# Summing softmax exponentials in place with an adding DMA, GpSimd adds and a fold, in a fused attention and feed-forward kernel

## Chip, cores and metric

The kernel runs on one core of one Trainium2 chip. The metric is device time in microseconds (us) of one execution; the program is launched once for the whole computation.

## What is computed

The reference is a pre-norm transformer block on `x` of 8 x 1024 x 512 in float32: differential attention with 16 heads, then a feed-forward part with ternary weights.

```python
qkv = layernorm(x) @ w_qkv                     # 16 heads of 32; q and k are split in halves of 16
a1 = softmax(q1 @ k1.T / sqrt(32)); a2 = softmax(q2 @ k2.T / sqrt(32))
out = (a1 - lam * a2) @ v                      # then RMS norm per head, norm_w, times 0.2
x = x + rearranged(out) @ wo
h = bitlinear(layernorm(x), w_fc) + gate * (x @ v.T @ fast_b.T @ u.T)
x = x + bitlinear(relu(h) ** 2, w_proj)
```

The change concerns the denominators of the two softmaxes: for each query, the sum over 1024 keys of the exponentials of one map.

## The kernel before

**Stages.** A first stage (to about 140 us of the span) normalises and projects batch 0 and prepares the ternary weights. The attention loop runs to about 4260 us. The feed-forward part takes the rest and is not touched.

**Units.** The attention loop is cut into NU = 256 units: batch, head, and half of the 1024 queries (HS = 512). 32 units make a batch. For one unit the scores stand with keys on the partitions: 8 chunks of 128 keys (`kc` = 0 to 7), two maps (`sm`) and 512 queries. The loop goes two chunks at a time, so a unit has four steps, called here by their first chunk: kc 0, 2, 4 and 6. I write (u, kc) for a step.

**What a step does**, in the order written by hand, which TensorE (PE), ScalarE (ACT), VectorE (DVE) and GpSimd (POOL) keep as it stands:

- `max_scores` (L207, L218): score products of the unit two ahead (AHEAD = 16 chunks), whose row maxima DVE takes out of three PSUM banks.
- `exp_scores` (L267, L273): for the unit itself, minus the maximum (from `nms`) plus the scores on PE, and the exponential on ACT into a tile `e` of 128 x 2 x 2 x 512 float32, 1 MB. One `e` tile holds the two chunks of a step, so a unit has four: e0 to e3, in the dictionary `e_of[u, kc // 2]`.
- `add_up` (L283, L285): GpSimd adds tiles into a separate tile `es`: es = e0 + e1 at kc 2, es += e2 at kc 4, es += e3 at kc 6.
- extra work, gathered in `posts`: at kc 0 a step of `fill` (for the next batch: normalised rows, transposes L137, values L145, projections L157), `max_turn` (L232: transposes the next unit's maxima and sends them through DRAM to `nms`), `heads_out` (L324: transposes and divides the results of an earlier unit), and `sums`. In the second half of a batch every fourth unit has one more projection at kc 4. Every fourth unit has an output projection of four units (`output_rows`, L383) at kc 4, one unit after `rms_apply` (L368 to L371) on GpSimd at kc 2.
- `values` (L290): the products with the values for the two chunks of the step before, that is, one step late.

**Sums.** `sums(v)` multiplies by a matrix of ones: `quarters` issues four small products of 256 columns for each part of 512 keys-by-query columns. A part is half a tile (one of two chunks). `es` is two parts; a unit that is `light` leaves e3 out of the GpSimd adds and sums it as two more parts on PE. Light are 17 of the last 32 units (the odd ones and the last three). `sums(v)` stands at (v + 2, 0), for light units at (v + 1, 2); `heads_out(v)` at (v + 3, 0), for light units at (v + 2, 0).

**Buffers.** Five `e` tiles and two `es` tiles are turned round in order: a new `e` tile is the one used five tiles before, and its writer waits until the last reader of that one is done. PSUM has three banks for the maxima, one for the values and four (`one_bank`) for all else. GpSimd issues no DMA in this loop; SyncE (SP) issues them all.

Of the kernel before, what the change touches and what calls it, by code (L numbers as in the profile page):

```python
# [8 lines left out]
F32 = mybir.dt.float32  # L9
F32R = mybir.dt.float32r  # L10
AF = mybir.ActivationFunctionType
ALU = mybir.AluOpType
# [5 lines left out]
P = 128  # L18
# [6 lines left out]
def block_phases(  # L25
# [14 lines left out]
    nc = tc.nc  # L40
    B, S, E = x.shape
    H, HD = norm_w.shape
# [3 lines left out]
    HS = S // 2  # L46
    SCALE = float(HD) ** -0.5
    NU = B * H * 2
# [55 lines left out]
    def one_bank():  # L104
        return ps_1.tile([P, 512], F32, tag="one", name="one")
# [71 lines left out]
    def load_keys(g):  # L177
        b, h = divmod(g, H)
        tk_of[g] = p_tk.tile([P, S], F32R, tag="tk", name="tk")
        src = qk_of[b][1, h * HD : (h + 1) * HD]  # L180
        for i in range(2):
            nc.sync.dma_start(
                tk_of[g][i::2].bitcast(F32), src[:, i : i + 1, :].to_broadcast([HD, 2, S])
            )

    def load_queries(u):
        b, h = divmod(u // 2, H)
        cols = slice((u % 2) * HS, (u % 2) * HS + HS)
        tq_of[u] = p_tq.tile([P, HS], F32R, tag="tq", name="tq")
        src = qk_of[b][0, h * HD : (h + 1) * HD, :, cols].rearrange("r i t -> (r i) t")  # L190
        for i in range(2):
            nc.sync.dma_start(tq_of[u][i::2].bitcast(F32), src)
# [37 lines left out]
    def max_turn(u):  # L230
        tr = one_bank()
        nc.tensor.transpose(tr[0:8, 0:P], nm2_of.pop(u), ident)  # L232

        def post():
            mt = p_s.tile([8, 2, P], F32R, tag="mt", name="mt", bufs=2)
            nc.vector.tensor_copy(mt[:, 0, :], tr[0:8, 0:P])
            nc.vector.tensor_sub(mt[:, 1, :], tr[0:8, 0:P], mt[:, 0, :].bitcast(F32))
            md = dpool.tile([2, 4, 2, P], F32, tag="md", name="md", bufs=4)
            nc.sync.dma_start(md.rearrange("s c a t -> (s c) a t"), mt.bitcast(F32))
            for sm in range(2):  # L240
                nc.sync.dma_start(
                    nms[u % 3][64 * sm : 64 * sm + 2].bitcast(F32)
                    .rearrange("a (c t) -> a c t", c=4),
                    md[sm].rearrange("c a t -> a c t"),
                )

        return post

    e_of, es_of, acc_of, avs_of = {}, {}, {}, {}

    def exp_scores(u, kc, between=None):

# [19 lines left out]

    def light(u):

        return u >= NU - 2 * H and (u % 2 == 1 or u >= NU - 3)

    def add_up(u, kc):
        e = e_of[u, kc // 2]  # L280
        if kc == 2:
            es_of[u] = p_es.tile([P, 2, 2, HS], F32, tag="es", name="es")
            nc.gpsimd.tensor_add(es_of[u], e_of[u, 0], e)  # L283
        elif kc == 4 or kc == 6 and not light(u):
            nc.gpsimd.tensor_add(es_of[u], es_of[u], e)  # L285

    def quarters(out, w, e, start, stop):

        for g in range(4):
            nc.tensor.matmul(  # L290
                out[32 * g : 32 * g + 32, :], w,
                e[:, g // 2, (g % 2) * (HS // 2) : (g % 2 + 1) * (HS // 2)],
                start=start, stop=stop,
            )
# [10 lines left out]
    def evict(u):  # L305
        avs_of[u] = p_s.tile([P, 2, HS // 2], F32, tag="avs", name="avs", bufs=4)

        nc.scalar.activation(avs_of[u][:, 0, :], acc_of.pop(u), AF.Copy, scale=one_nlam)

    def sums(u):  # L310
        ps = one_bank()
        es = es_of.pop(u)
        parts = [t[:, i] for t in ((es, e_of[u, 3]) if light(u) else (es,)) for i in range(2)]
        for i, part in enumerate(parts):
            quarters(ps[:, 0 : HS // 2], ones, part, i == 0, i == len(parts) - 1)
        return lambda: nc.scalar.copy(avs_of[u][:, 1, :], ps[:, 0 : HS // 2])
# [39 lines left out]
    def rms_squares(n):  # L356
        sq_of[n] = p_y.tile([P, 4, P], F32, tag="sq", name="sq")
        nc.scalar.activation(sq_of[n], og_of[n], AF.Square)
# [16 lines left out]
    def output_rows(n, bank=one_bank):  # L375
        b, hp = divmod(n, NHP)
        xr = p_y.tile([P, E], F32, tag="xr", name="xr")
        rows = x[b].rearrange("(d r) e -> r d e", d=HD)
        for r in range(4):
            nc.sync.dma_start(xr[32 * r : 32 * r + 32, :], rows[4 * hp + r])  # L380
        py = bank()
        for c in range(KC):
            nc.tensor.matmul(  # L383
                py, og_of[n][:, c, :], wo_sb[:, c, :],
                start=(c == 0), stop=(c == KC - 1),
            )

        def post():
            y = p_y.tile([P, E], F32, tag="y", name="y")
            nc.vector.scalar_tensor_tensor(y, py, nw[:, hp : hp + 1], xr, ALU.mult, ALU.add)  # L390
            nc.sync.dma_start(x1_dram[n // 4][n % 4], y)

        return post
# [39 lines left out]
    def whole(step):  # L433
        post = step()
        if post:
            post()
# [3 lines left out]
    with tc.tile_pool(name="a_stage", bufs=1) as stage, tc.manual_schedule(engines=engines):  # L440
# [26 lines left out]
        for i, step in enumerate(steps):  # L467
# [4 lines left out]
            posts = [step()]  # L472
# [7 lines left out]
            if i >= heads:  # L480
                um, im = divmod(i - heads, NS)
# [71 lines left out]

    adds, outs = {}, {}
    for v in range(NU):
        adds.setdefault((v + 1, 2) if light(v) else (v + 2, 0), []).append(v)
        outs.setdefault((v + 2, 0) if light(v) else (v + 3, 0), []).append(v)
    done = None
    ctx.enter_context(tc.manual_schedule(engines=engines))
    with tc.tile_pool(name="a_e", bufs=5) as p_e, tc.tile_pool(name="a_es", bufs=2) as p_es:  # L560
        for s in range(0, NS * NU + 2, 2):
            u, kc = divmod(s, NS)
            um, im = divmod(s + AHEAD, NS)
            if done is not None:
                evict(done)
                done = None
            if u > NU - 2 * H and kc == 0:
                prep.fetch()
            if um < NU:
                if im == 0 and um + 1 < NU:  # L570
                    if um % 2 == 1:
                        load_keys(um // 2 + 1)
                    load_queries(um + 1)
                between, first = max_scores(um, im, apart=True)
            else:
                between = first = None
            if u < NU:
                if u % (2 * H) == 0 and kc == 0:
                    assert not fill
                    fill = prepare(u // (2 * H) + 1) if u + 2 * H < NU else prepare_tokens()  # L580
                exp_scores(u, kc, between=between)
                if first:
                    first()
                exp_scores(u, kc + 1)
                add_up(u, kc)
            reduce = max_scores(um, im + 1) if um < NU else None
            posts = []

            if fill and (kc == 0 or kc == 4 and u % (2 * H) >= H and u % 4 == 0):
                prepare_step, long = fill.pop(0)  # L590
            else:
                prepare_step = None
            if prepare_step and long:
                posts.append(prepare_step())
            if kc == 0 and um <= NU:
                posts.append(max_turn(um - 1))
            for v in outs.pop((u, kc), []):
                posts.append(heads_out(v))
                if v % 4 == 3:
                    n = v // 4  # L600
                    later[u, 6] = lambda n=n: rms_squares(n)
                    later[u + 1, 0] = lambda n=n: rms_sums(n)
                    later[u + 1, 2] = lambda n=n: rms_apply(n)
                    later[u + 2, 4] = lambda n=n: output_rows(n)
            if (u, kc) in later:
                posts.append(later.pop((u, kc))())
            for v in adds.pop((u, kc), []):
                posts.append(sums(v))
            if prepare_step and not long:
                posts.append(prepare_step())  # L610
            if reduce:
                reduce()
            if 2 <= s < NS * NU + 2:
                uv, kv = divmod(s - 2, NS)
                values(uv, kv)
                values(uv, kv + 1)
                if kv == NS - 2:
                    done = uv
            for post in posts:
                if post:  # L620
                    post()
        evict(done)
        prep.fetch_rest()
        whole(lambda: sums(NU - 1))
    assert not later and list(adds.values()) == list(outs.values()) == [[NU - 1]]

# [439 lines left out]
```

## Time and profile before

| | |
|---|---|
| median of 3 runs | 5345.61 us (5343.15 to 5349.25) |
| profiled execution: its own time | 5346.45 us |
| profiled execution: span of its instructions | 5344.5 us |
| granted TensorE clock | 0.999 |
| busy in the span: PE, DVE, ACT, POOL | 99%, 71%, 53%, 77% |
| DMA | 328.49 MB, mean 61 GB/s |

The profiler gives each instruction's start and duration. A group in the page is a line, an engine and an operation with its tiles, its count, its busy time and the mean of one in ns, then the idle time before it and what ended that. PE time is modelled for the ends of the matmuls, so 99% doesn't mean that PE has no slack. A timeline row is start, duration, engine, line, operation, tiles and shape. I divide the attention loop by batch: seven first halves (units 0 to 15 of batches 0 to 6), with transposes and values for the next batch as fill; seven second halves, with projections as fill; and the last batch, nearly without fill.

### The profile page before, as it was taken

Reading aid. Unit: us, or ns where it says so; the run is one execution under the profiler, and the core shown is the slowest. Engines: PE = TensorE matmul, PEld = TensorE weight load, DVE = VectorE, ACT = ScalarE, POOL = GpSimd, SP = SyncE. Lnnn points to the kernel's source line nnn. Section 1 sums busy time; section 2 is a strip of 40 time slices with the busy share of each in tenths; the row PEclk is TensorE's granted clock in tenths of the full one; section 3 lists DMA queues with packets and bytes.
Section 4 is the critical chain, followed back from the end, with each engine's and each line's share of the span. In section 5 each row is a group of like instructions: output and inputs, shape, how many; then the busy total and the mean of one; then the engine's idle time right before and its main releaser. Section 6 shows DMA issues by size and latency. Waiting matters only on the chain.

```text
span 5344.5 us, 105614 instructions
## 1 busy us (share of the span) xinstructions
PE 5277.1 (99%) x41522; PEld 3244.8 (61%) x41522; DVE 3786.5 (71%) x7599; ACT 2834.1 (53%) x5502; POOL 4128.1 (77%) x1511
## 2 busy tenths in 40 slices
PE   8999999999999999999999999999999999999999
PEld 4555555555555555555555555555555588788887
DVE  6877787777778777877777777777888545555554
ACT  4665566566656665666566656655666522222221
POOL 0998899889988998899899989998888733333333
PEclk9999999999999999999999999999999999999999
DMA  8112211221121112111211121112211101111111
GB/s 275 49 52 77 69 51 54 75 71 50 55 79 63 52 55 77 64 55 59 77 59 53 63 74 61 52 65 77 97 48 47 60 18 32 32 32 32 32 32 32
DMA packets 185247, 328.49 MB, mean 61 GB/s; under 512 B 33312, under 2 KB 55840, under 8 KB 184112
## 3 DMA queue, kind: packets, MB, share of 16 engines
q1 hardware_dynamic: 183824, 319.12, 18.7%
q8 instruction: 329, 5.39, 0.4%
q0 software_dynamic: 544, 2.10, 0.1%
q14 instruction: 166, 1.36, 0.1%
q10 hardware_dynamic: 384, 0.52, 0.0%
HBM read 209.16 MB, written 112.46 MB: 60 GB/s over the span
## 4 chain that ended last, share of the span: by engine, by line
PE 80%; POOL 12%; DVE 2%; issue 2%; ACT 1%; DMA 1%; SPq 0%; POOLq 0%; DVEq 0%; ACTq 0%
PE acc L290 15%; PE one L267 13%; PE mx L207 12%; PE one L157 8%; PE y L722 7%; POOL es L285 7%; PE pf L708 7%; PE one L290 4%; PE one L145 4%; PE one L383 3%; POOL es L283 3%; PE one L324 2%; DVE nm L218 1%; PE pf L709 1%; ACT e L273 1%
## 5 line engine op out<-in xcount | busy, mean ns | idle before, releaser
L218 DVE TENSOR_REDUCE nm<-mx 128x1 f32<-128x512 f32 x4096 | 2548.4, 682 | 257.6 <-PE mx L207 252.1
L273 ACT ACTIVATE e<-one 128x512 f32<-128x512 f32 x4096 | 2116.8, 602 | 802.8 <-PE one L267 750.5
L285 POOL TENSOR_TENSOR es<-es,e 128x2048 f32<-128x2048 f32 x495 | 2262.6, 4571 | 62.0 <-ACT e L273 30.0
L207 PE MATMUL mx<-tk,tq 64*128 64x512 f32 x4096 | 1451.2, 444 | 6.7 <-DVE nm L218 5.5
L283 POOL TENSOR_TENSOR es<-e 128x2048 f32<-128x2048 f32 x256 | 1170.0, 4570 | 277.1 <-ACT e L273 277.1
L267 PE MATMUL one<-nms,one 64*128 64x512 f32 x4096 | 1177.4, 420 | 4.6 <-ACT e L273 2.7
L290 PE MATMUL acc<-e,v 128*32 128x256 f32 x16384 | 1092.6, 384 | 0.0
L207 PEld LDWEIGHTS mx<-tk,tq 64*128 64x128 f32 x4096 | 751.0, 184 | 546.9 <-DVE nm L218 311.5
L267 PE MATMUL one<-tq,tk 64*128 64x512 f32 x4096 | 1065.0, 393 | 0.0
L712 POOL TENSOR_TENSOR r<-r 128x512 f32<-128x512 f32 x256 | 269.0, 1052 | 644.4 <-ACT r L711 636.7
L290 PEld LDWEIGHTS acc<-e,v 128*32 128x32 f32 x16384 | 450.1, 109 | 433.7 <-issue 177.3
L267 PEld LDWEIGHTS one<-tq,tk 64*128 64x128 f32 x4096 | 580.4, 185 | 83.2
L711 ACT ACTIVATE r<-pf,s_fc 128x512 f32<-128x512 f32 x256 | 176.5, 689 | 793.1 <-PE pf L709 555.8
L267 PEld LDWEIGHTS one<-nms,one 64*128 64x128 f32 x4096 | 515.8, 184 | 79.9 <-DVE og L347 14.7
L722 PE MATMUL y<-wpr,r 128*128 128x512 f32 x2048 | 523.7, 397 | 3.3 <-DVE r L716 1.5
L715 DVE CAST r<-r 128x512 fp32r<-128x512 f32 x256 | 179.0, 699 | 421.9 <-POOL r L712 421.8
L157 PE MATMUL one<-hT,wqk 128*128 128x512 f32 x1024 | 472.8, 605 | 0.0
L722 PEld LDWEIGHTS y<-wpr,r 128*128 128x128 f32 x2048 | 374.8, 188 | 98.6 <-DVE o L732 20.1
L708 PE MATMUL pf<-hTh,wfc 128*128 128x512 f32 x1024 | 399.3, 390 | 0.0
L708 PE MATMUL pf<-hTl,wfc 128*128 128x512 f32 x1024 | 398.9, 390 | 0.0
L165 DVE SCALAR_TENSOR_TENSOR pc<-one,pc 128x512 fp32r<-128x512 f32 x128 | 88.5, 691 | 344.4 <-ACT pc L164 344.4
L157 PEld LDWEIGHTS one<-hT,wqk 128*128 128x128 f32 x1024 | 184.1, 189 | 213.9 <-issue 186.4
(133 smaller groups left out, 4291.6 us busy)
## 6 DMA issues: line engine op xcount, KB each, us to landing
qk<-pc SPq DMA_DIRECT2D x128, 512.0 KB
tk<-qk SPq DMA_DIRECT2D x256, 256.0 KB
tq<-qk SPq DMA_DIRECT2D x512, 128.0 KB
xs<-in_L_attn_x SPq DMA_DIRECT2D x64, 256.0 KB
xr<-in_L_attn_x SPq DMA_DIRECT2D x256, 64.0 KB
x_dram<-y SPq DMA_DIRECT2D x64, 256.0 KB
out<-o SPq DMA_DIRECT2D x248, 64.0 KB
nms<-md SPq DMA_DIRECT2D x512, 4.0 KB
```

The costliest lines, as they stand in the source:

```text
L145: nc.tensor.matmul(pv, hT_of[b][:, kc, c * P : (c + 1) * P], wv[:, kc, :], start=(kc == 0), stop=(kc == KC - 1),)
L157: nc.tensor.matmul(ps, wqk[:, kc, c0 : c0 + P], hT_of[b][:, kc, tok], start=(kc == 0), stop=(kc == KC - 1),)
L207: nc.tensor.matmul(mx[sm], tq[rows, c * P : (c + 1) * P], tk[rows, kh * 512 : kh * 512 + 512], start=True, stop=True,)
L218: nc.vector.tensor_reduce(nm_of[u][:, kh, sm, c : c + 1], mx[sm], AX.X, ALU.max, negate=True)
L267: nc.tensor.matmul(st[sm], w[rows, cols], m[rows, :], start=(w is one2), stop=(w is not one2))
L273: nc.scalar.activation(e[:, kc % 2, sm, :], st[sm], AF.Exp)
L283: nc.gpsimd.tensor_add(es_of[u], e_of[u, 0], e)
L285: nc.gpsimd.tensor_add(es_of[u], es_of[u], e)
L290: nc.tensor.matmul(out[32 * g : 32 * g + 32, :], w, e[:, g // 2, (g % 2) * (HS // 2) : (g % 2 + 1) * (HS // 2)], start=start, stop=stop,)
L708: nc.tensor.matmul(pf, w[:, kc, :], hT, start=(kc == 0 and i == 0), stop=False)
L712: nc.gpsimd.tensor_mul(r, r, r)
L722: nc.tensor.matmul(ys[i], r2[:, i * P : (i + 1) * P], prep.wpr[j // (NJ // 2)][:, j % (NJ // 2), :], start=(j == 0 and k == 0), stop=(j == ...
```

## The change

`add_up` no longer uses a tile of its own. For most units, e1 += e0 is done at (u, 4) by a DMA that adds into its destination, issued by GpSimd. At (u, 6) GpSimd adds e2 += e3, then e2 += e1 (after the DMA has landed), then folds e2's second chunk onto its first. `sums` then has one part of four products instead of two. Light are only the last five units: they have e1 += e0 at kc 4 and e2 += e1 at kc 6 on GpSimd, and four parts on PE. `add_up` now stands at the end of the step behind `values`, since the in-place adds overwrite what `values` reads. `sums(v)` moves from (v + 2, 0) to (v + 1, 6), `heads_out(v)` from (v + 3, 0) to (v + 2, 0), and with it the RMS norm and the output projection by one unit. There are seven `e` tiles and no `es` tiles. Within kc 0, `heads_out` and `max_turn` go ahead of the fill step.

```diff
-        return u >= NU - 2 * H and (u % 2 == 1 or u >= NU - 3)
+        return u >= NU - 5
     def add_up(u, kc):
-        e = e_of[u, kc // 2]
-        if kc == 2:
-            es_of[u] = p_es.tile([P, 2, 2, HS], F32, tag="es", name="es")
-            nc.gpsimd.tensor_add(es_of[u], e_of[u, 0], e)
-        elif kc == 4 or kc == 6 and not light(u):
-            nc.gpsimd.tensor_add(es_of[u], es_of[u], e)
+        if kc == 4:
+            if light(u):
+                nc.gpsimd.tensor_add(e_of[u, 1], e_of[u, 1], e_of[u, 0])
+            else:
+                nc.gpsimd.dma_start(e_of[u, 1], e_of[u, 0], accum_op=ALU.add)
+        elif kc == 6:
+            e = e_of[u, 2]
+            if not light(u):
+                nc.gpsimd.tensor_add(e, e, e_of[u, 3])
+            nc.gpsimd.tensor_add(e, e, e_of[u, 1])
+            if not light(u):
+                nc.gpsimd.tensor_add(e[:, 0], e[:, 0], e[:, 1])
...
-        es = es_of.pop(u)
-        parts = [t[:, i] for t in ((es, e_of[u, 3]) if light(u) else (es,)) for i in range(2)]
+        parts = [e_of[u, 2][:, 0]]
+        if light(u):
+            parts += [e_of[u, 2][:, 1], e_of[u, 3][:, 0], e_of[u, 3][:, 1]]
...
-        adds.setdefault((v + 1, 2) if light(v) else (v + 2, 0), []).append(v)
-        outs.setdefault((v + 2, 0) if light(v) else (v + 3, 0), []).append(v)
+        adds.setdefault((v + 1, 2) if light(v) else (v + 1, 6), []).append(v)
+        outs.setdefault((v + 2, 0), []).append(v)
...
-    with tc.tile_pool(name="a_e", bufs=5) as p_e, tc.tile_pool(name="a_es", bufs=2) as p_es:
+    with tc.tile_pool(name="a_e", bufs=7) as p_e:
...
                 exp_scores(u, kc + 1)
-                add_up(u, kc)
...
-            if prepare_step and long:
-                posts.append(prepare_step())
-            if kc == 0 and um <= NU:
-                posts.append(max_turn(um - 1))
             for v in outs.pop((u, kc), []):
                 posts.append(heads_out(v))
...
+            if kc == 0 and um <= NU:
+                posts.append(max_turn(um - 1))
+            if prepare_step and long:
+                posts.append(prepare_step())
...
                 values(uv, kv + 1)
                 if kv == NS - 2:
                     done = uv
+                if u < NU:
+                    add_up(u, kc)
```

## The prediction on record

> **What bounds the kernel now.** I read the page's busy shares first, then busy time by window for one cycle of four units in each of the three kinds of stage, then the GpSimd and TensorE timelines of a cycle.
>
> The windows' columns are start:end, length, busy time of each engine with instruction counts, granted clock, DMA share, GB/s. The rows are a first half, a second half, and the last batch.
>
> ```profile
> 1268.90:1331.20 62.30, 62.30 (x566) 35.30 (x565) 49.39 (x102) 40.64 (x79) 60.97 (x22) 1.00 0.17 53
> 991.00:1061.80 70.80, 70.80 (x582) 39.68 (x584) 50.91 (x104) 39.98 (x79) 58.84 (x15) 1.00 0.23 76
> 4070.50:4128.70 58.20, 56.99 (x574) 33.22 (x576) 47.66 (x99) 37.20 (x74) 49.88 (x14) 1.00 0.16 48
> ```
>
> TensorE is full in all three. GpSimd (fifth figure) is full too in the first half, 60.97 of 62.30, and has room in the other two. So work taken off TensorE pays only where GpSimd lets it.
>
> GpSimd in the first half, from the timeline:
>
> ```profile
> 1292.22 4.52 POOL L283 TENSOR_TENSOR es<-e 128x2048 f32<-128x2048 f32 x1
> 1296.82 0.20 POOL L368 TENSOR_SCALAR ss<-ss 128x16 f32<-128x16 f32 x1
> 1297.11 2.92 POOL L369 TENSOR_TENSOR ss<-ss,neg_half 128x16 f32<-128x16 f32 x1
> 1300.11 1.05 POOL L371 TENSOR_TENSOR og<-og,ss 128x512 f32<-128x512 f32 x1
> 1301.12 9.19 POOL L285 TENSOR_TENSOR es<-es,e 128x2048 f32<-128x2048 f32 x2
> ```
>
> Three adds of 4.6 us a unit, and in every fourth unit 4.3 us of RMS norm between them.
>
> TensorE in one unit with only transposes as fill, from its timeline:
>
> ```profile
> 1274.13 0.50 PE L207 MATMUL mx<-tk,tq 64*128 64x512 f32 x1
> ...
> 1275.84 1.07 PE L290 MATMUL acc<-e,v 128*32 128x256 f32 x16
> 1276.84 0.49 PE L207 MATMUL mx<-tk,tq 64*128 64x512 f32 x1
> ...
> 1278.54 0.27 PE L232 MATMUL one<-ident,nm 128*8 128x128 f32 x1
> 1278.81 0.66 PE L324 MATMUL one<-ident,avs 128*128 128x128 f32 x4
> 1279.39 1.07 PE L290 MATMUL one<-es,ones 128*32 128x256 f32 x16
> 1280.40 0.66 PE L137 MATMUL one<-ident,xs 128*128 128x128 f32 x4
> 1280.98 1.07 PE L290 MATMUL acc<-e,v 128*32 128x256 f32 x16
> ```
>
> From row starts: a bare step is 1276.84 - 1274.13 = 2.71 us, of which `values` ends the last 1.0. The sums of two parts take 1280.40 - 1279.39 = 1.0 us, so one part costs 0.5. `max_turn` and `heads_out` take 0.85, a transpose of fill 0.6. A unit is 10.8 + 0.85 + 1.0 = 12.65 us, plus fill: 0.6 (transposes), 3.4 (values), 3.6 (projection), 3.4 (output projection).
>
> **The change, part by part.**
>
> *Sums on TensorE.* The page has 4096 + 272 = 4368 matmuls of L290 into `one`, 8 to a part: 546 parts. After: 251 units with one part, five with four: 271. 275 parts go, at 0.5 us: 137 us if all of it is on the path. By stage: 8 us per half batch for each of 14 halves (112), 25.5 us in the last batch.
>
> *GpSimd instructions.* A unit had three adds, 13.7 us. Now two adds, a fold, a DMA issue. The fold has 1024 elements a partition; between the rows of 512 elements (1052 ns, L712) and 2048 (4571 ns) the slope is 2.29 ns, so 2.25 us. The nearest issue rows are 0.98 and 0.76 us (`wv`, `wo_sb`, 1 MB each, early in the span). Together 12.4 us.
>
> *The new chain.* This is what gives back part of the gain. The first add needs e3, whose exponentials end 0.2 us behind the step (an ACT row of four at 2000.24, 2.06 us long, in a step that ends at 2002.11); with the hand-over I take 0.3. So with unit end as zero: 0.3 + 4.57 + 4.6 + 2.25 = 11.75 us, and `sums` at (u + 1, 6) can't start before 11.8. Behind it TensorE's in-order queue holds 0.5 us of sums, 1.0 of values, and the next unit's scores. So **no unit is shorter than 13.3 us**. A unit with a projection is 15.4 on TensorE after the change and waits for nothing; one with transposes alone (12.75) is held up 0.55 us; one without fill (12.15) 1.15 us. Before, sums stood two steps after the last add and had that time free.
>
> *The adding DMA.* X is the time from its issue to its landing. It is issued behind the values of (u, 4), or behind the former chain and the RMS norm where these run late, and the second add waits for it. Nothing in this trace adds by DMA. The lower bound is 0.98 + 4.57 = 5.55 us, since the first add is queued between issue and use: a faster DMA gains nothing more. The nearest rows are the two GpSimd loads:
>
> ```profile
> wv<-in_L_attn_w_qkv POOLq DMA_DIRECT2D x1, 1024.0 KB, 8.3
> wo_sb<-in_L_attn_wo POOLq DMA_DIRECT2D x1, 1024.0 KB, 13.1
> ```
>
> In the first, the trace has the first packet 3.85 us after the issue, and other loads on the same engines while it moved. The DMA table of that stretch shows 367 to 426 GB/s when full, which is 2.6 us for 1 MB: 6.5 us without company. In the attention loop the DMA share is only 0.16 to 0.23, so **I take X = 6.5**. If adding reads both operands one after the other it is 3.85 + 2 x 2.6 = 9.1, the upper end.
>
> The Trainium skill, "Collectives: The Full Stack", in Part 3 under "The bandwidth ceiling", speaks against the change: an adding transfer reads two sources through one ring and runs at half the rate of a copy. With the packets of this trace that is the 9.1 above; no run here shows an adding DMA yet. By the skill's fit for a GpSimd DMA ("DMA: Bandwidth & Descriptors", Anatomy of one DMA), 2.0 us plus bytes at 436 GB/s, X would be an estimated 4.4 us for a copy and 6.8 with both reads; the 3.85 us to the first packet here disagrees with its 2.0. By 4.4 the sum would be the floor below, by 6.8 some 15 us above my forecast.
>
> *GpSimd as a cycle.* When it runs late, a unit costs it X from issue to second add, then 4.6 + 2.25. Four units: 4X + 27.4, plus 4.3 of RMS norm, plus in first halves 2.2 for two sets of statistics (three rows, 1.1 us each). So 4X + 33.9 in first halves, 4X + 31.7 elsewhere.
>
> *Light units, reordering, buffers.* The last batch loses its light units; that is in the counts. At the very end an add of 4.6 us now follows the last exponentials, with one step of values as cover: +3 us. `heads_out` and `max_turn` ahead of the projection let VectorE do its 1.8 us of extra work under it; before, 70.80 of 70.80 busy on TensorE shows no stall there: 0. In the last batch two `heads_out` met in one step and VectorE held TensorE up (58.20 against 56.99); that goes. Seven tiles in place of five and two: the next writer of e0's buffer is the exponential of (u + 1, 6), some 8 us after the adding DMA is due: 0. On SP nothing is added; the transfers of `nms` meet the adding DMA, with most of a unit to spare.
>
> **Sum at the floor, X up to 5.55.** Second halves: 4 units 70.8 to 68.8; 7 x 8 = -56 us. First halves: the four kinds of unit become 13.3 (transposes, held), 15.6 (values), 16.2 (transposes and output projection), 15.7: 60.8 against 62.3; 28 cycles x 1.5 = -42. Last batch: three units at 13.3; in the fourth the RMS norm has delayed the DMA's issue to 11.75 + 4.3 = 16.05, then 0.9 + 4.57 + 4.6 + 2.25 = 28.4, plus 1.6 = 30.0, less the 13.3 of the unit before, 16.7. 56.6 against 58.2, 8 cycles: -13. End: +3. Together **-108 us**.
>
> **At X = 6.5.** First halves need 59.9 on GpSimd against 60.8, so it fits, but not evenly: its 13.35 us a unit meets units of 13.3, and lateness after the RMS norm isn't made good at once. I put 0.7 us a cycle (between 0 and the 1.5 saved): +20. Last batch: 57.7 against 56.6, 8 cycles: +9. So -108 + 29 = -79. The profiled execution took 5346.45 us, 0.8 above the median shown: 5346.45 - 79 = 5267 us, and with a few us for meetings on the DMA engines **5270 us**.
>
> **Rivals.**
>
> *The adding DMA is slow (slower than before).* Beyond X of about 6.7 GpSimd sets first halves and last batch: 28 x (4X + 33.9 - 62.3) + 8 x (4X + 31.7 - 58.2) = 144X - 1007, less 56, plus 3. It decides from **X = 7.4**. With X = 8.3, the `wv` row as it stands: +135 us, 5481. With 9.1: +250, 5597. For it: that row, and the second read. Against it: the row's company on the engines.
>
> *The adding DMA is quick.* X at 5.55 or less: 5238 us. For it: the early row may carry what a first use costs. Against it: nothing in this trace lands faster from GpSimd.
>
> *It doesn't overlap as it says.* If GpSimd stood still until the landing, a unit would cost X + 4.57 + 6.85 = 17.9; first halves 78 us a cycle, over +440 us. Against it: the second issue (18.86) follows the first (17.87) by 1 us, long before the landing.
>
> **How the numbers follow.** A change under 0.2% (11 us) can't be told from none. X up to 5.55: 0.18. X to about 7.3, still faster by over 0.2%: 0.38, my forecast among them. Within 0.2%: 0.06. Slow DMA: 0.35, of which 0.13 above X = 8.4. No overlap: 0.03. Faster 0.56, same 0.06, slower 0.38. The range 5225 to 5500 leaves out 0.16 above and a little below; faster cases alone lie between 5225 and 5335.
>
> **What would show it.** Right: one-part sums waiting for GpSimd in units without projections, and none in the others; adds of e2 and e1 that wait under 1 us for the DMA; second-half cycles of 68.8 us; DMA issue to landing about 6.5. Wrong: second adds idle for 2 us or more on the DMA in every first-half unit, and first-half cycles over 62.3; or a fold far from 2.25 us; or TensorE waiting on `nms` or `tq`.

## The result, and the profile after

The changed kernel takes **5619.56 us** (median of 5 runs, 5613.40 to 5635.59) against 5346.15 us: 1.0516 times the time before, 95% interval 1.0504 to 1.0528. It is slower by 273 us, where 5270 us (76 us faster) was forecast; the time also lies above the forecast's range of 5225 to 5500. The profiled execution took 5617.27 us, its span 5615.5 us, with a granted clock of 0.98 (0.999 before).

From the page of the changed kernel: span, busy shares, the DMA queue of GpSimd, the chain that ended last (by engine), five groups (busy time and mean ns, then idle time and what ended it), and the adding DMA's issues with the median time to landing. L290 is e2 += e3, L291 is e2 += e1, L293 the fold, L298 the values and sums.

```profile
span 5615.5 us, 102081 instructions
PE 5296.7 (94%) x39322; PEld 3184.9 (57%) x39322; DVE 3790.6 (68%) x7599; ACT 2822.0 (50%) x5502; POOL 3856.2 (69%) x1774
q0 software_dynamic: 36688, 265.31, 24.1%
PE 58%; DMA 19%; POOL 18%; issue 2%; DVE 1%; ACT 1%; POOLq 0%; SPq 0%; DVEq 0%; ACTq 0%
L291 POOL TENSOR_TENSOR e<-e 128x2048 f32<-128x2048 f32 x256 | 1171.4, 4576 | 514.3 <-DMA e<-e 513.6
L290 POOL TENSOR_TENSOR e<-e 128x2048 f32<-128x2048 f32 x251 | 1170.6, 4664 | 224.5 <-PE acc L298 183.6
L293 POOL TENSOR_TENSOR e<-e 128x1024 f32<-128x1024 f32 x251 | 594.6, 2369 | 19.7
L298 PE MATMUL one<-e,ones 128*32 128x256 f32 x2168 | 186.9, 425 | 256.8 <-POOL e L293 232.7
e<-e POOLq DMA_DIRECT2D x251, 1024.0 KB, 8.3
```

GpSimd is less busy than before (69% for 77%) and TensorE too (94% for 99%): both wait. GpSimd's second add waits 514 us in all for the adding DMA, and TensorE's sums wait 233 us for the fold that comes after it. 19% of the last chain is DMA time. The landing took 8.3 us, and the sums have the 2168 products that the counts asked for (271 parts).

A window of one first half in the changed kernel (start:end, length, busy times of PE, PEld, DVE, ACT, POOL, granted clock, DMA share, GB/s):

```profile
1269.00:1339.00 70.00, 60.07 (x508) 32.74 (x501) 47.88 (x101) 38.72 (x76) 55.62 (x29) 0.95 0.44 105
```

Before, TensorE and GpSimd were both full here, 62.30 and 60.97 of 62.30. Now neither is, and the clock is down to 0.95. From it, first GpSimd's timeline of one unit and the start of the next, then the row of TensorE that waits for the fold:

```profile
1303.72 0.91 POOL L286 DMA_DIRECT2D e<-e  x1 [0.18 <-issue]
1304.38 4.81 POOL L290 TENSOR_TENSOR e<-e 128x2048 f32<-128x2048 f32 x1
1312.53 4.60 POOL L291 TENSOR_TENSOR e<-e 128x2048 f32<-128x2048 f32 x1 [3.34 <-DMA e<-e]
1317.20 2.36 POOL L293 TENSOR_TENSOR e<-e 128x1024 f32<-128x1024 f32 x1
1319.51 0.87 POOL L286 DMA_DIRECT2D e<-e  x1
1321.31 4.58 POOL L290 TENSOR_TENSOR e<-e 128x2048 f32<-128x2048 f32 x1 [0.93 <-PE acc L298]
1328.03 4.58 POOL L291 TENSOR_TENSOR e<-e 128x2048 f32<-128x2048 f32 x1 [2.14 <-DMA e<-e]
```

```profile
1319.62 0.64 PE L298 MATMUL one<-e,ones 128*32 128x256 f32 x8 [1.58 <-POOL e L293]
```

From issue to second add it is 8.8 us (1303.72 to 1312.53), of which the first add covers 4.8; then 4.6 and 2.4 us, and only then is the next DMA issued. TensorE stands 1.6 us in front of the sums, with the next scores queued behind them.

Where the time went, by stage (a unit ends with its last values; profiled executions, minus before; the second column is from the prediction's working, at X = 6.5):

| stage | forecast | measured | without the wait for the landing (e1, below) |
|---|---|---|---|
| first halves, batches 0 to 6 | -42 + 20 | +199 | +3 |
| second halves, batches 0 to 6 | -56 | +22 | -32 |
| last batch | -13 + 9 | +48 | -4 |
| start, end, feed-forward | +3 | +2 | +5 |

### The profile page after: what moved, and what is told of

Read it like the earlier page. It is cut to its first block, busy times and chain, and to the rows that moved or that the text cites. A ratio compares the mean times of both kernels' runs of the same rounds, so it can differ in the third digit from the quotient of the medians.

```text
span 5615.5 us, 102081 instructions
## 1 busy us (share of the span) xinstructions
PE 5296.7 (94%) x39322; PEld 3184.9 (57%) x39322; DVE 3790.6 (68%) x7599; ACT 2822.0 (50%) x5502; POOL 3856.2 (69%) x1774
## 4 chain that ended last, share of the span: by engine, by line
PE 58%; DMA 19%; POOL 18%; issue 2%; DVE 1%; ACT 1%; POOLq 0%; SPq 0%; DVEq 0%; ACTq 0%
DMA e<-e 18%; POOL e L291 10%; PE acc L298 9%; PE y L732 8%; PE pf L718 8%; PE one L267 8%; PE mx L207 8%; PE one L157 6%; POOL e L293 5%; PE one L145 3%; PE one L298 2%; PE one L392 2%; PE one L333 1%; POOL ss L378 1%; PE pf L719 1%
## 5 line engine op out<-in xcount | busy, mean ns | idle before, releaser
L291 POOL TENSOR_TENSOR e<-e 128x2048 f32<-128x2048 f32 x256 | 1171.4, 4576 | 514.3 <-DMA e<-e 513.6
L207 PE MATMUL mx<-tk,tq 64*128 64x512 f32 x4096 | 1475.1, 449 | 5.3 <-DVE nm L218 2.6
L290 POOL TENSOR_TENSOR e<-e 128x2048 f32<-128x2048 f32 x251 | 1170.6, 4664 | 224.5 <-PE acc L298 183.6
L267 PE MATMUL one<-nms,one 64*128 64x512 f32 x4096 | 1216.4, 430 | 26.6 <-DVE og L356 17.9
L298 PE MATMUL acc<-e,v 128*32 128x256 f32 x16384 | 1126.6, 394 | 0.0
L267 PE MATMUL one<-tq,tk 64*128 64x512 f32 x4096 | 1082.9, 398 | 0.0
L298 PEld LDWEIGHTS acc<-e,v 128*32 128x32 f32 x16384 | 463.4, 111 | 539.9 <-issue 290.0
L267 PEld LDWEIGHTS one<-tq,tk 64*128 64x128 f32 x4096 | 595.0, 189 | 87.4
L293 POOL TENSOR_TENSOR e<-e 128x1024 f32<-128x1024 f32 x251 | 594.6, 2369 | 19.7
L267 PEld LDWEIGHTS one<-nms,one 64*128 64x128 f32 x4096 | 520.5, 189 | 132.9 <-PE mx L207 22.7
L298 PE MATMUL one<-e,ones 128*32 128x256 f32 x2168 | 186.9, 425 | 256.8 <-POOL e L293 232.7
```

The lines of the kernel that those rows point to most:

```text
L207: nc.tensor.matmul(mx[sm], tq[rows, c * P : (c + 1) * P], tk[rows, kh * 512 : kh * 512 + 512], start=True, stop=True,)
L267: nc.tensor.matmul(st[sm], w[rows, cols], m[rows, :], start=(w is one2), stop=(w is not one2))
L290: nc.gpsimd.tensor_add(e, e, e_of[u, 3])
L291: nc.gpsimd.tensor_add(e, e, e_of[u, 1])
L293: nc.gpsimd.tensor_add(e[:, 0], e[:, 0], e[:, 1])
L298: nc.tensor.matmul(out[32 * g : 32 * g + 32, :], w, e[:, g // 2, (g % 2) * (HS // 2) : (g % 2 + 1) * (HS // 2)], start=start, stop=stop,)
```

## The experiments

Fifteen kernels ran. Each is compared with the kernel before on the same chip; ratios are to that, with their 95% interval. Line numbers are those of each run's own kernel. Step lengths are medians over the trace, from the start of one step's values to the start of the next's, for the steps kc 0, 2, 4, 6 of a unit; before, a second-half unit without output projection had 7.77, 2.71, 2.71, 2.71 us. X is a DMA's time from issue to landing.

### Is it the wait for the landing?

**e1: no wait.** The second add takes e3 once more in place of e1; the DMA still runs.

```diff
-            nc.gpsimd.tensor_add(e, e, e_of[u, 1])
+            nc.gpsimd.tensor_add(e, e, e_of[u, 1 if light(u) else 3])
```

> The second add reads e3 again in place of e1, so that it waits for no DMA; the adding DMA is still issued in the same place, and the first two tiles are left out of the denominators (e3 counts twice). Theory 1 (the landing of the adding DMA, 8.25 us after its issue, sets GpSimd's cycle, and TensorE's waits behind it halve its clock for a while): the 514 us of waits of the second add go, first halves fall from 276 to about 244 us and the time to 5230 to 5280 us. Theory 2 (the traffic of the adding DMA slows the rest): the time stays above 5550 us. Theory 3 (the chain of three GpSimd instructions behind the last exponential and the early place of the sums cost by themselves): between 5350 and 5500 us.

5316.38 us, 0.9939 (0.9924 to 0.9954), clock 0.996. The DMA moved as many bytes with a mean X of 8.5 us. So the wait is the cause of the loss, 303 us of it (5619.56 - 5316.38), and contention of the transfer with other work is not. But the floor is -31 us, not -108: that part of the forecast fails by itself.

**e2: half the bytes.** Only the first chunk is added by the DMA, 512 KB.

```diff
-                nc.gpsimd.dma_start(e_of[u, 1], e_of[u, 0], accum_op=ALU.add)
+                nc.gpsimd.dma_start(e_of[u, 1][:, 0], e_of[u, 0][:, 0], accum_op=ALU.add)
```

> The DMA adds only the first chunk of e0 onto that of e1, 512 KB in place of 1 MB (e0's second chunk is left out of the denominators). Theory 1: issue to landing falls from 8.25 to about 5 us, under the 5.5 us that the issue and the first add take anyway, and the time to 5230 to 5290 us, as with no wait at all. Theory 2: half the traffic, so about half of the loss is left, 5450 to 5520 us. Theory 3: 5350 to 5500 us.

5346.65 us, 0.9999 (0.9990 to 1.0008), mean X 5.6. Half the traffic brings back all of the loss and not half of it. But the time is above the 5230 to 5290 expected: that expectation still counted on the forecast's floor, and the second adds still wait 62 us in all for the DMA.

**e3: a copy in place of the add.** The same bytes, without `accum_op`.

```diff
-                nc.gpsimd.dma_start(e_of[u, 1], e_of[u, 0], accum_op=ALU.add)
+                nc.gpsimd.dma_start(e_of[u, 1], e_of[u, 0])
```

> The DMA copies e0 over e1 and doesn't add (e1 is left out of the denominators, e0 takes its place). This measures the price of adding: in the changed kernel the first packet comes 1.45 us after the issue and the packets of 8 KB take 639 ns against 313 ns for packets of that size of plain loads. If adding costs a second read, issue to landing falls from 8.25 to 4.5 to 5.5 us, and by theory 1 the time to 5230 to 5290 us. If a copy from SBUF to SBUF is as slow as the adding one, both stay: 8 us and about 5600 us.

5341.98 us, 0.9991 (0.9982 to 1.0001). Its issues in the page:

```profile
e<-e POOLq DMA_DIRECT2D x251, 1024.0 KB, 5.3
```

5.3 us against the adding DMA's 8.3. In the trace (medians), from first packet to last, a copy moves for 3.7 us and an add for 6.1; an 8 KB packet takes 321 and 639 ns. The first packet follows the issue by 1.2 and 1.5 us. That settles the size of X: a short lead, packets that take twice as long, and some 1.7 times the movement. With X near 5.5 the time is that of the kernel before (e2 and e3); so even the quick-DMA rival's 5238 us would not have come.

The rule that the prediction weighed (the Trainium skill, "Collectives: The Full Stack", Part 3, "The bandwidth ceiling": two source reads, half the rate) agrees with 639 against 321 ns a packet; the whole movement, 6.1 against 3.7 us, is less than doubled.

**e7: the DMA's add on GpSimd.** The part of the change that uses the DMA is undone, the rest stays.

```diff
-                nc.gpsimd.dma_start(e_of[u, 1], e_of[u, 0], accum_op=ALU.add)
+                nc.gpsimd.tensor_add(e_of[u, 1], e_of[u, 1], e_of[u, 0])
```

> The DMA alone is undone: GpSimd does e1 += e0 itself, the rest is the changed kernel. GpSimd then has three adds and a fold, 16.2 us a unit, 64.8 + 6.9 = 71.7 us for four units of a first half (69.2 in the changed kernel) and 69.1 in the last batch (65.3). Theory 1: a little slower than the changed kernel, 5640 to 5700 us. If the adding DMA were worse than the add that it replaces: under 5600 us.

5739.43 us, 1.0735 (1.0719 to 1.0751), clock 0.971; 40 us above what I expected. The DMA is 120 us better than the add that it replaces. With three adds and a fold, 16.1 us, GpSimd needs more than most units of TensorE last.

### Can the wait be hidden?

**e4: sums where they were before.**

```diff
-        adds.setdefault((v + 1, 2) if light(v) else (v + 1, 6), []).append(v)
-        outs.setdefault((v + 2, 0), []).append(v)
+        adds.setdefault((v + 1, 2) if light(v) else (v + 2, 0), []).append(v)
+        outs.setdefault((v + 2, 0) if light(v) else (v + 3, 0), []).append(v)
```

> Sums go back to (v + 2, 0) and heads_out to (v + 3, 0), as before the change; the rest is the changed kernel. Theory 1: GpSimd's cycle doesn't depend on it, so first halves stay near 275 us; but TensorE no longer holds its values, for which the next unit's first add waits, behind the sums, and second halves lose their waits: 5500 to 5590 us, with fewer stretches of half clock. Theory 3: the early place is the cause, 5300 us or less.

5589.28 us, 1.0450 (1.0435 to 1.0466). Its waits (us in all, times, longest):

```profile
POOL e L291 <- DMA e<-e: 561.8, 251, 5.4
ACT e L273 <- DMA e<-e: 253.3, 70, 7.9
ACT e L273 <- POOL e L291: 178.8, 90, 2.8
```

The sums no longer wait, and the time hardly moves, since GpSimd's cycle itself is too long. The exponentials now wait in the sums' place, for a buffer that the late DMA or add still holds. The wait went round to the next engine in the ring.

**e5: fold first.** The fold doesn't need the DMA; it goes ahead of the wait, and e1's two chunks come last, half as wide. All three of these adds stand on L295 of its kernel, and the adding DMA on L286.

```diff
-            nc.gpsimd.tensor_add(e, e, e_of[u, 1])
-            if not light(u):
-                nc.gpsimd.tensor_add(e[:, 0], e[:, 0], e[:, 1])
+            if light(u):
+                nc.gpsimd.tensor_add(e, e, e_of[u, 1])
+            else:
+                for part in (e[:, 1], e_of[u, 1][:, 0], e_of[u, 1][:, 1]):
+                    nc.gpsimd.tensor_add(e[:, 0], e[:, 0], part)
```

> Same DMA, same additions, other order: behind e2 += e3 GpSimd folds e2 first, and then adds the two chunks of e1 onto its first chunk. 2.4 us of work move from behind the landing to ahead of it: 4.6 + 2.4 = 7.0 us beside the transfer, 4.8 us behind it in place of 7.0. Theory 1 (GpSimd's cycle is issue to landing plus what stands behind it): the cycle of a unit falls from 15.6 to about 13.3 us, under TensorE's, the second adds' waits fall from 514 to under 150 us, and the time to 5310 to 5380 us. If something else about the DMA's wait counts (its place in the queue, or meetings with other transfers), over 5480 us.

5376.48 us, 1.0056 (1.0041 to 1.0071), clock 0.995. Order alone brings back 243 of 273 us. The wait for the DMA, and a unit in GpSimd's timeline:

```profile
POOL e L295 <- DMA e<-e: 76.6, 82, 4.7
```

```profile
1288.98 0.93 POOL L286 DMA_DIRECT2D e<-e  x1
1289.64 4.87 POOL L290 TENSOR_TENSOR e<-e 128x2048 f32<-128x2048 f32 x1
1294.59 2.37 POOL L295 TENSOR_TENSOR e<-e 128x1024 f32<-128x1024 f32 x1
1297.74 4.82 POOL L295 TENSOR_TENSOR e<-e 128x1024 f32<-128x1024 f32 x2 [0.78 <-DMA e<-e]
```

Between issue and use lie 4.9 + 2.4 us in place of 4.9, and behind the landing 4.8 in place of 7.0. From issue to the end of the chain it is 13.6 us.

**e6: fold first and late sums.** e5 with e4's two lines.

> As e5_fold_first, with the sums at (v + 2, 0) and heads_out at (v + 3, 0) as before the change. In e1_no_landing, where nothing waits for the DMA, the step kc 2 of units without long fill grew from 2.7 to 3.4 us: I take it that the sums at kc 0 had covered VectorE's extra work. If so, the steps kc 2 return to 2.7 to 2.9 us, and the time is 15 to 50 us under that of e5_fold_first. If the early place costs nothing, the two agree within 10 us.

5409.10 us, 1.0120 (1.0103 to 1.0137), 33 us over e5: a miss. Second halves do gain (-30 us against before, -18 in e5), but first halves lose 51 us and the last batch 38: the exponentials wait 164 us for buffers that the DMA holds, and output projections stand 70 us behind exponentials. At 729.42, for example, one has waited 4.4 us for an exponential that itself waited 5.3 us for the DMA. The steps kc 2 of odd first-half units 5 to 11 fall only from about 3.5 to between 3.0 and 3.5 us, so the guess about VectorE's cover was right in part.

**e11: light units as before.** The last batch's 17 light units come back.

```diff
-        return u >= NU - 5
+        return u >= NU - 2 * H and (u % 2 == 1 or u >= NU - 3)
```

> The changed kernel with light units as they were before the change (17 of the last 32, which need neither the DMA nor the fold, and have four parts). Theory (the last batch lost 48 us because every one of its units waits for the landing): the last batch comes back to within 15 us of before, the rest stays, 5560 to 5595. Rival (the last batch lost for another reason, such as the earlier place of the sums): it stays at 5610 or more.

5592.00 us, 1.0458 (1.0444 to 1.0473). The last batch's loss goes from 48 to 25 us, not to within 15; the rest stays. The wait for the landing explains half of that stage.

**e12: fold first and light units as before.**

> Both repairs: folding first, so that the landing has half of e2 to e3's adds more time, and light units as before the change. Theory: the 5376 of folding first less its 17 us in the last batch, 5350 to 5368, the same as before or slightly slower; what stays is the first halves' 31 us. Rival (light units between others cost more than they save, since four parts are 1.5 us of TensorE each): 5376 or more.

5375.93 us, 1.0056 (1.0042 to 1.0070), the same as e5: the rival. When the wait is nearly gone, four parts cost a light unit what it saves (last batch +20 against +17 us).

### What does a wait cost?

In the trace of the changed kernel TensorE's clock is halved in 55 stretches of mostly 3.4 or 6.8 us, 224 us in all (before: 3, 15 us). Of the 55, 50 begin in a wait of TensorE of over 1.5 us, or within 1.4 us behind one. Of 24 gaps of 1.5 to 2 us, 7 have such a stretch, of 34 of 2 to 3 us 23, of 23 longer ones 20. By estimate, if all of that time is work at half the rate, up to 112 of the 273 us could be clock.

**e8: waits filled.** Three or six unread products of 256 columns ahead of the sums in units that wait, into the unused half of their bank.

```diff
         ps = one_bank()
+        for _ in range(0 if light(u) or (u < NU - 2 * H and (u + 1) % (2 * H) >= H) else (0, 3, 0, 6)[(u + 1) % 4]):
+            nc.tensor.matmul(
+                ps[:, HS // 2 :], ident, wo_sb[:, 0, 0 : HS // 2], start=True, stop=True,
+            )
```

> Ahead of the sums of every second unit of first halves and the last batch, TensorE does three or six more products of 256 columns that nobody reads (1.3 or 2.6 us), where it waits for GpSimd 1.6 and 3.2 us on the mean in the changed kernel. In that one 55 stretches of half the clock, 224 us together, start at the waits. If they cost time of their own, the half-clock time falls to under 130 us and the time by 20 to 70 us, though TensorE has more to do. If they fall into waits and cost nothing, the time stays within 15 us or grows.

5597.54 us, 1.0467 (1.0451 to 1.0483), clock 0.992, half-clocked stretches 86 us (these two from the profiled execution, the fastest of four at 5583.52 us). TensorE does more, and the time falls by 22 us. So the halved clock costs time of its own; as the half-clocked stretches fell by 138 us and the time by only 22, I take it that most of them lay where the cycle of GpSimd set the pace anyway; no run shows that by itself.

The Trainium skill ("TensorE: Matmul & The Clock Gate", Part 1, "The HAM clock gate") has the clock halved after an idle window of about 3.4 us; here 23 of 34 waits of 2 to 3 us were already followed by a half-clocked stretch.

### What is one part worth, and what the new order?

e1 left two terms of the forecast in doubt: 0.5 us for each part, and nothing for the order at kc 0. e9, e10 and e13 take the kernel before and add one thing each; e14 adds two.

**e9: a fold in second halves,** where GpSimd had room; sums two steps later, as before.

```diff
+    def folded(u):
+        return u < NU - 2 * H and u % (2 * H) >= H
...
+            if kc == 6 and folded(u):
+                es = es_of[u]
+                nc.gpsimd.tensor_add(es[:, 0], es[:, 0], es[:, 1])
...
-        parts = [t[:, i] for t in ((es, e_of[u, 3]) if light(u) else (es,)) for i in range(2)]
+        parts = [t[:, i] for t in ((es, e_of[u, 3]) if light(u) else (es,)) for i in range(1 if folded(u) else 2)]
```

> The kernel before, with one thing of the change put where GpSimd has room: in the second halves of batches 0 to 6, behind the last add at kc 6, GpSimd folds the second chunk of the sum onto the first, so these units' sums have one part; their place, two steps later, stays. Theory (one part less is worth about 0.3 us a unit, the step at kc 0 going from 7.77 to about 7.5 us, as in the runs with late sums): 112 units, -30 us, about 5316; GpSimd goes from 58.8 to 68.4 of 70 us a cycle there and just fits. Rival (it is so full that its lateness is not made good): sums wait for the fold, half-clock stretches appear, 5340 or more. My prediction's 0.5 us a part would give 5290.

5380.21 us, 1.0064 (1.0050 to 1.0078): slower, by the number the rival's, but not by its way: TensorE's sums hardly wait for GpSimd (7 us in all). Second halves: the step at kc 0 falls from 7.77 to 7.34 us, and the step at kc 2 grows from 2.71 to 3.14. VectorE shows why. First TensorE's projection and its next scores, then VectorE's rows around the same step, in the kernel before and then in e9:

```profile
1577.94 3.70 PE L157 MATMUL one<-hT,wqk 128*128 128x512 f32 x8
...
1583.98 0.49 PE L207 MATMUL mx<-tk,tq 64*128 64x512 f32 x1
...
1582.31 0.69 DVE L165 SCALAR_TENSOR_TENSOR pc<-one,pc 128x512 fp32r<-128x512 f32 x1 [3.05 <-ACT pc L164]
...
1584.56 2.47 DVE L218 TENSOR_REDUCE nm<-mx 128x1 f32<-128x512 f32 x4
```

```profile
1587.29 3.70 PE L157 MATMUL one<-hT,wqk 128*128 128x512 f32 x8
...
1592.90 0.50 PE L207 MATMUL mx<-tk,tq 64*128 64x512 f32 x1
...
1591.66 0.69 DVE L165 SCALAR_TENSOR_TENSOR pc<-one,pc 128x512 fp32r<-128x512 f32 x1 [3.06 <-ACT pc L164]
...
1593.91 2.47 DVE L218 TENSOR_REDUCE nm<-mx 128x1 f32<-128x512 f32 x4
```

The projection begins at 1577.94 and 1587.29; VectorE waits for its end, then does the rows of `max_turn` and `heads_out`, and begins the next maxima 6.62 us after the projection's start in both kernels. TensorE comes to its next scores 0.43 us earlier in e9, and has to wait there until VectorE frees a bank of maxima. Before, TensorE had no stall in this stage, and yet VectorE came back just in time: it had no slack.

First halves lose 31 us, all in their first units. ScalarE's timeline there (e9; L286 is the first add, es = e0 + e1):

```profile
1198.74 4.03 ACT L273 ACTIVATE e<-one 128x512 f32<-128x512 f32 x8 [3.06 <-POOL es L286]
```

GpSimd is full in the second half (busy 246.12 of 250 us in a window of it, for 219.41 before). In the first two units behind the border its first add starts 5.2 to 5.4 us later against TensorE's steps than it did before, and an exponential waits 3 us for a tile that it still reads.

**e10: the new order alone.**

```diff
-            if prepare_step and long:
-                posts.append(prepare_step())
-            if kc == 0 and um <= NU:
-                posts.append(max_turn(um - 1))
             for v in outs.pop((u, kc), []):
                 posts.append(heads_out(v))
...
+            if kc == 0 and um <= NU:
+                posts.append(max_turn(um - 1))
+            if prepare_step and long:
+                posts.append(prepare_step())
```

> The kernel before with the change's order of extra work alone: heads_out and max_turn ahead of the fill step at kc 0. Theory: it is worth nothing by itself, 5340 to 5355. Rival: it is part of the loss or of the gain in the second halves, over 10 us either way, seen in the steps at kc 0 and kc 2.

5380.93 us, 1.0063 (1.0051 to 1.0076). Each long step at kc 0 is 0.21 us longer: `max_turn`, `heads_out` and the projection take 4.38 us to the start of the sums (1588.41 to 1592.79) where they took 4.18 (1577.94 to 1582.12). The rival is right: the order is not worth "nothing". Why it costs 0.21 us, no run shows.

**e13: the fold stops four units before the border.** e9, with:

```diff
-        return u < NU - 2 * H and u % (2 * H) >= H
+        return u < NU - 2 * H and H <= u % (2 * H) < 2 * H - 4
```

> As the kernel with the fold in second halves, but folding only in units 16 to 27 of a batch, so that GpSimd has four units to catch up before the next first half. Theory (its loss of 35 us was GpSimd's lateness carried over the border; a part by itself is worth nothing, since VectorE then ends 0.43 us late in the step at kc 2): 5340 to 5352, the same as before. Rival (the fold costs in every unit): 5370 or more.

5345.32 us, 0.9999 (0.9990 to 1.0008). The loss at the border is gone, and the part that goes is still worth nothing.

**e14: fold and order together.** e13, with the new order in the steps that have one-part sums.

```diff
+            ahead = kc == 0 and u < NU and folded(u - 2)
-            if prepare_step and long:
+            if prepare_step and long and not ahead:
                 posts.append(prepare_step())
-            if kc == 0 and um <= NU:
+            if kc == 0 and um <= NU and not ahead:
                 posts.append(max_turn(um - 1))
...
+            if ahead and um <= NU:
+                posts.append(max_turn(um - 1))
+            if prepare_step and long and ahead:
+                posts.append(prepare_step())
```

> As the kernel whose fold stops early, and in the steps at kc 0 that have one-part sums heads_out and max_turn stand ahead of the fill step. Theory (fold and order need each other: VectorE's extra work goes under the projection, and the 0.5 us of the part really goes, less the 0.21 us that the order costs): 0.28 us in each of 84 units, -23 us, 5315 to 5330, faster than before by 0.4%. Rival (they are independent: 0 and +0.21 us): 5360 or so.

5323.00 us, **0.9956 (0.9944 to 0.9968)**: faster than the kernel before and the changed one, with nothing left out of the sums. TensorE's next scores and VectorE's rows in e14, where the projection begins at 1569.83:

```profile
1574.89 0.50 PE L207 MATMUL mx<-tk,tq 64*128 64x512 f32 x1
...
1570.30 0.24 DVE L340 RECIPROCAL rc<-one 128x4 f32<-128x4 f32 x2
...
1574.19 0.69 DVE L165 SCALAR_TENSOR_TENSOR pc<-one,pc 128x512 fp32r<-128x512 f32 x1 [2.10 <-ACT pc L164]
1575.42 2.48 DVE L218 TENSOR_REDUCE nm<-mx 128x1 f32<-128x512 f32 x4 [0.54 <-PE mx L207]
```

The rows of `heads_out` and `max_turn` now run under the projection; the maxima begin 5.59 us after its start, and wait for TensorE, not TensorE for them. The part's time really goes, 0.43 us (7.55 us against e10's 7.98 at kc 0), less 0.21 for the order, and kc 2 stays at 2.7: second halves -22.7 us, 84 units of 0.27. Alone, the part is worth 0 in these units (e13) and the order some +18 us by estimate (84 times 0.21; +36 in all of e10's units); together they are worth -23.

**e15: e12 with the old order.** The fill step goes ahead of `max_turn` and `heads_out` again.

> The changed kernel folding first, with light units as before the change, and with the fill step ahead of max_turn and heads_out again, as before the change. Theory (with no sums at kc 0, VectorE's 1.8 us of extra work there has no cover left but the new order): steps at kc 2 grow by some 0.9 us in second halves, 5376 + 70 to 100 us, 5430 to 5480. Rival (the order is independent, worth 0.21 us the other way): 5376 less 40 us, 5335.

5428.82 us, 1.0153 (1.0137 to 1.0168), 53 us slower than e12, a little under the expected interval. In second halves kc 2 grows from 2.71 to 3.6 us. The changed kernel needs its order.

## Why the prediction was wrong

**The step that failed: "I take X = 6.5".** The `wv` row said 8.3, and I stripped 1.8 us off it as company on the engines. The adding DMA took 8.3 (mean 8.25, 90% between 7.0 and 10.1). Both pieces of my estimate were off, in opposite directions: 1.5 us to the first packet, not 3.85 (the rival on a quick DMA had suspected a first use behind that; in the changed kernel even the first adding DMA has 1.5, and no run tests what held up the early load), and 6.1 us of movement, not 2.6, of which a copy takes 3.7 and the adding brings the rest (e3). I had worked out the doubling, 9.1 us, and kept it only as the upper end. The rival "the adding DMA is slow" decides from 7.4 us, and it is what happened; e1 shows that the wait, not the traffic, is the price. Of the 350 us between forecast and result, some 270 are this step (303 us for the wait, where X = 6.5 was to cost 29), and 77 are the floor (below).

**The cycle on GpSimd** was the right mechanism, a little too short. In first halves X was 8.0 us on average (8.6 in second halves); the forecast's 4X + 33.9 then gives 65.9 us for a cycle of four units, and GpSimd's trace has 68.2 from issue to issue. Hand-over, second add and fold come to 7.2 us a unit, not 6.85, which is 1.3 of the 2.3 us; the rest is left for idle time. By the ends of units the six whole first halves took 277.3 us on average, 69.3 a cycle (62.2 before). The fold itself was well bounded, 2.37 us for 2.25.

**What the slow rival had too low: its 5481.** By stage it gave 134 us in first halves (199 measured), -56 in second (+22), +54 in the last batch (+48). The second halves are its largest miss. There it used the floor, as if a late chain had no place to show. Of the four cycles of a half, the first three took what they took before (-0.8 to +1.6 us, forecast -2), since the sums held up two units of four (15.9 and 16.2 us for 15.6 in e1), and the last one 3.2 us more on average. The half-clocked stretches come on top; they were not in the forecast at all. How much of the 273 us is clock I can only bound by estimate, between the 22 us that e8 shows and 112.

**The floor: -108 forecast, -31 shown (e1).** Second halves gave -32 for -56: "so one part costs 0.5" is nearly right for TensorE's rows (0.43, e14 against e10), but the edit that was costed at 0, the order, costs 0.21 a unit (e10). That order was no free extra: without it VectorE's cover is gone and the part is worth nothing (e9, e13, e15). "70.80 of 70.80 busy on TensorE shows no stall there: 0" was the wrong reading: no stall does not say how much slack the engine behind has. First halves gave +3 for -42. In e1 a steady cycle gains 0.6 to 1.0 us, not 1.5. In odd units 5 to 11, which have only transposes as fill, kc 2 grows from between 2.7 and 3.2 us to between 3.6 and 3.7; VectorE's extra rows used to lie under two parts of sums at kc 0, and none are left there:

```profile
1313.72 0.28 DVE L237 TENSOR_TENSOR mt<-one,mt 8x128 fp32r<-8x128 f32 x1
1313.93 2.46 DVE L218 TENSOR_REDUCE nm<-mx 128x1 f32<-128x512 f32 x4
```

In that step (e1) values begin at 1311.47, and the maxima start 2.5 us later (1.5 in e14, 1573.91 to 1575.42). The first half of batch 0 loses 5 us. In batches 1 to 6 the first four units lose 2.3 us and the other twelve win 2.6; what makes the first ones late is open, as no run was made for it. One figure of the working doesn't follow from its terms: a unit with a projection is 15.4 us there, where 12.15 + 3.6 gives 15.75. The trace before has 15.9, less one part, so 15.4 is the better one, and no sum rests on it.

**What was right.** The counts of parts; the bound from GpSimd's cycle, and that it decides in first halves and the last batch; and that GpSimd doesn't stand still until a landing (in the two units shown the first add begins 0.7 and 1.8 us after the issue, 1.7 on average). Of the signs of being wrong, first-half cycles over 62.3 us came; second adds idle for 2 us or more came in 57 of 112 first-half units (2.1 us on average), not in every one.

**Seven tiles** were costed at 0, and with late sums that fails: e4's exponentials wait 253 us for the DMA and 179 us for the add behind it. With early sums, exponentials wait 11 us in all for such an add and not for the DMA.

## What to carry to other kernels

Put all work that doesn't need a transfer between its issue and its use, before you count on its time: here folding ahead of the wait was worth 243 us. Price an adding transfer as two reads, from a row with nothing stripped off. And when an engine is 100% busy, ask how late the next one already is: work taken off the first pays only as far as the second has slack, so edits that look independent may need each other.

## What the runs showed of the hardware

A transfer of 1 MB from SBUF to SBUF, issued by GpSimd, took 5.3 us to land as a copy and 8.3 us as an add; 8 KB packets took 321 and 639 ns (medians; changed kernel and e3). Halving the bytes of the add brought it to 5.4 us (median, e2). In the changed kernel TensorE's granted clock fell to half, mostly for 3.4 or 6.8 us, at 23 of 34 waits of 2 to 3 us and at 20 of 23 longer ones; with unread products in the gaps (e8) the half-clocked time fell from 224 to 86 us.
